# The queries' squares in the output norm: added by GpSimd ahead of the channel sums, or summed by TensorE as groups of their own

## The chip, the cores and the metric

The kernel runs on one core of a Trainium2 chip. The metric is device time in microseconds (us): the median of three runs. The core's engines are TensorE (PE in the profile, with PEld for its weight loads), VectorE (DVE), ScalarE (ACT), GpSimd (POOL) and SyncE (SP), which issues the DMAs. Each engine takes its instructions in the order in which the program lists them, and waits on semaphores for the others.

## The reference: what is computed

Two layers over 1,024 tokens of width 256 (two sequences of 512). Layer 0 is a gated delta rule attention (16 key heads, 32 value heads, head width 128) and a feed-forward layer with ternary weights; layer 1 is an attention with 16 small heads, a ternary feed-forward layer and a mixture of 8 experts. The change lies in the normalisation of layer 0's attention output. Cut to what matters:

```
def _l2norm(x, eps=1e-06):
    return x * jax.lax.rsqrt(jnp.sum(x * x, -1, keepdims=True) + eps)
...
q = _l2norm(q) * Dk ** (-0.5)
k = _l2norm(k)
...
o = _chunk_gated_delta_rule(q, k, v, g, beta)
og = o * jax.nn.silu(z)
og = og * jax.lax.rsqrt(jnp.mean(og * og, -1, keepdims=True) + EPS) * norm_w
return og.reshape(B, T, -1) @ W_out
```

The attention is linear in q, so the kernel never normalises q: it scans with the raw q and takes q's length out in the last norm. With z for the unnormalised `og`, the factor of a token and a value head is then the inverse square root of mean(z*z) plus a constant times (sum of q*q plus a small number). So the sum over the 128 channels of z squared and a scaled sum over the channels of q squared are needed together, for each token and each value head; two value heads share one q.

## The kernel before

Everything is laid out with channels on the 128 partitions and the 512 tokens of a sequence along the free axis. Layer 0's attention is a loop over 16 key heads `h`; a head has two sequences (`seqs`), and a sequence has two units (`s.units`), its value heads. An iteration holds stages of several heads:

- for head `h + 2`: the keys' projection and convolution (`keys_pre`), their norms and decays (`keys`: GpSimd's `rk`, `affine_select` on `e`, and the product `nt<-nt,e` of 128x512), a round trip through DRAM (`base_load`, into `nb`), and `base`, the inversion of 32x32 blocks by 31 steps of two GpSimd instructions each (`xtmp<-xc,nb`, `xc<-xc,xtmp`);
- for head `h + 1`: `inverse`, which fetches those blocks through DRAM (`scr`, `xt`) and joins them into 128x128 inverses with small TensorE products (`bank<-xb,nt` first), and `weights`, which splits the projection weights in a high and a low part (GpSimd makes `wzl`, `wvl`, `wql`, `wkl`);
- for head `h`: projections and convolutions of queries and values, GpSimd's `qg<-qg,q`, the four chunks of `scan`, and `finish`;
- for head `h - 1`: `project` (GpSimd's `ftok`, the inverse square root) and `output`, the product with `W_out`, added into `acc` by VectorE.

`finish` is where the change is. ScalarE squares q in place (with the scale that carries the constant) and writes the squares of each unit's z into a tile `zsq`. Then TensorE sums over the 128 channels by multiplying with ones: the PSUM bank `ps` has 128 rows, 64 for each sequence and in them 32 for each unit, all 32 holding the same sum. Two groups with 64 columns of ones put each sequence's q sum in its 64 rows (`start=True, stop=False`), and four groups with 32 columns add each unit's z sum to its 32 rows. VectorE copies the bank to `zrow`, TensorE transposes it in four pieces, and VectorE makes `tot` from one row of each 32, which GpSimd raises to the power -1/2 (`ftok`).

The order of instructions on each engine isn't the order of this text. All calls go to a recorder (`Plan`), which knows the dependencies and has a cost for every instruction. It then runs a list scheduler many times (`ROUNDS`): each time it places the instructions by priority (the longest path to the end) on the five engines, gives tiles their slots in SBUF and PSUM banks to the groups, keeps the best order that it found, and moves some of the tiles to other slots at random (`SEED`) before the next. The best order is what is issued, from one place, line 572; so every row of the profile has that line, and tiles' names tell the operations apart. TensorE's consecutive matmuls inside `with unit(nc):` are one piece that the scheduler doesn't break up.

Of the kernel before, what the change touches and what calls it, by code (L numbers as in the profile page):

```python
# [42 lines left out]
ALU = mybir.AluOpType  # L43
# [51 lines left out]
def unit(nc):  # L95
    return nc.unit() if isinstance(nc, Plan) else nullcontext()
# [26 lines left out]
class Plan:  # L123
# [7 lines left out]

    BANKS, EARLY, LONG = 8, 3, 4
    CAPS = {"conv": 2}
    ROUNDS, SEED = 120, 9
    SLOTS = (32, 44), (128, 5), (544, 1), (1024, 14), (2048, 50), (3072, 2), (4096, 19), (8192, 3)

    def __init__(self, g):
# [666 lines left out]
def layer0(g, acc, a):  # L804

    nc, tc = g.nc, g.tc
    w_qkvz, w_out = a["w_qkvz"], a["w_out"]
    U = 2 * NC
    with ExitStack() as st:
# [76 lines left out]
        def started(h):  # L886
            seqs = heads[h] = [Seq() for b in range(B)]
            for b, s in enumerate(seqs):
                s.b, s.h, s.units = b, h, []
            return seqs  # L890
# [225 lines left out]
        def finish(h, seqs):  # L1116


            ps = g.psum("lv")
            for s in seqs:  # L1120
                nc.scalar.activation(s.q, s.q, AF.Square, scale=math.sqrt(1e-6) * P)
                for u in s.units:
                    u.sq = ul.tile([P, T], F32, tag="vb", name="zsq", bufs=6)
                    nc.scalar.activation(u.sq, u.z, AF.Square)
            with unit(nc):
                for s in seqs:
                    d = slice(64 * s.b, 64 * s.b + 64)
                    nc.tensor.matmul(ps[d], g.ones[:, :64], s.q, start=True, stop=False)
                for s in seqs:
                    for u in s.units:  # L1130
                        d = 64 * s.b + 32 * u.r
                        nc.tensor.matmul(ps[d : d + 32], g.ones[:, :32], u.sq, start=False, stop=True)
            rows = ul.tile([P, T], F32, tag="a", name="zrow", bufs=2)
            nc.vector.tensor_copy(rows, ps)
            ps = g.psum("lv")
            with unit(nc):
                for c in range(NC):
                    d = slice(c * P, (c + 1) * P)
                    nc.tensor.transpose(ps[:, d], rows[:, d], g.ident)
            tot = ul.tile([P, B, 2, NC], F32, tag="tot", name="tot", bufs=2)  # L1140
            heads = ps.rearrange("p (c b r x) -> p b r c x", c=NC, b=B, r=2)[:, :, :, :, 0]
            nc.vector.tensor_scalar(tot, heads, 1.0 / P, 1e-12 * P, op0=ALU.mult, op1=ALU.add)
            return tot
# [56 lines left out]
        for h in range(HK):  # L1200
            cur = heads[h]
            if h + 2 < HK:
                seqs = started(h + 2)
# [15 lines left out]
            for s in cur:  # L1219
                t = slice(s.b * T, (s.b + 1) * T)  # L1220
                s.z = yl.tile([P, 2, T], F32, tag="z", name="z", bufs=4)
                for u in s.units:
                    ps = g.psum("z")
# [25 lines left out]
            if h:  # L1249
                output(h - 1, done[0], f)  # L1250
            done = cur, finish(h, cur)
            del heads[h]
        output(HK - 1, cur, project(HK - 1, *done))
# [554 lines left out]
```

## Time and profile before

| | us |
|---|---|
| runs | 1270.39, 1272.55, 1276.15 |
| median | 1272.55 |
| the profiled execution, its own time | 1273.35 |
| its span, first to last instruction | 1271.2 |

| engine | busy us | share of span | instructions |
|---|---|---|---|
| TensorE | 1201.5 | 95% | 10452 |
| VectorE | 980.0 | 77% | 2266 |
| ScalarE | 889.1 | 70% | 2347 |
| GpSimd | 794.0 | 62% | 1419 |

The busy shares are averages over the whole span. The page's strip of 40 slices (each about 32 us, the digit is the busy share in tenths) shows how they lie in time:

```profile
PE   5598889999999999999999999999999989999998
POOL 4355777787867878778586858668662366042432
```

The head loop takes the slices from about the sixth to the thirty-second; before it come the gates and the first feed-forward layer, after it layer 1. The four largest groups of GpSimd in the page are its two block-inversion rows, the product `nt<-nt,e` and the small powers:

```profile
L572 POOL TENSOR_TENSOR xtmp<-xc,nb 128x126 f32<-128x126 f32 (+22 forms) x496 | 177.0, 357 | 80.8 <-DMA nb<-scr 21.5
L572 POOL TENSOR_TENSOR xc<-xc,xtmp 128x126 f32<-128x126 f32 (+22 forms) x496 | 186.7, 376 | 31.1
L572 POOL TENSOR_TENSOR ftok<-tot,half 128x16 f32<-128x16 f32 x16 | 46.6, 2912 | 40.1 <-DVE tot L572 40.0
```

After the bar stand the busy time in us and the mean of one in ns; after the next bar the idle time of the engine just before these instructions, and what ended most of it.

### The profile page before, as it was taken

Reading aid. Unit: us, or ns where it says so; the run is one execution under the profiler, and the core shown is the slowest. Engines: PE = TensorE matmul, PEld = TensorE weight load, DVE = VectorE, ACT = ScalarE, POOL = GpSimd, SP = SyncE. Lnnn points to the kernel's source line nnn. Section 1 sums busy time; section 2 is a strip of 40 time slices with the busy share of each in tenths; the row PEclk is TensorE's granted clock in tenths of the full one; section 3 lists DMA queues with packets and bytes.
Section 4 is the critical chain, followed back from the end, with each engine's and each line's share of the span. In section 5 each row is a group of like instructions: output and inputs, shape, how many; then the busy total and the mean of one; then the engine's idle time right before and its main releaser. Section 6 shows DMA issues by size and latency. Waiting matters only on the chain.

```text
span 1271.2 us, 29063 instructions
## 1 busy us (share of the span) xinstructions
PE 1201.5 (95%) x10452; PEld 987.6 (78%) x10452; DVE 980.0 (77%) x2266; ACT 889.1 (70%) x2347; POOL 794.0 (62%) x1419
## 2 busy tenths in 40 slices
PE   5598889999999999999999999999999989999998
PEld 4498777778788888878888888888788777575687
DVE  7975667878897987979888897989776799274363
ACT  6767878687868878776787777777766245756641
POOL 4355777787867878778586858668662366042432
PEclk8799789999999999999999999999999989998999
DMA  6225113234143332332333242333333000000221
GB/s 183 86 66 142 35 35 91 51 92 110 51 109 69 83 77 77 98 84 76 84 84 83 62 110 50 102 80 82 69 89 87 21 9 11 7 6 10 64 68 34
DMA packets 160239, 89.83 MB, mean 71 GB/s; under 512 B 110560, under 2 KB 142368, under 8 KB 160096
## 3 DMA queue, kind: packets, MB, share of 16 engines
q1 hardware_dynamic: 160096, 87.97, 27.3%
q8 instruction: 83, 1.36, 0.4%
q14 instruction: 60, 0.49, 0.1%
HBM read 78.07 MB, written 9.73 MB: 69 GB/s over the span
## 4 chain that ended last, share of the span: by engine, by line
PE 68%; DVE 15%; ACT 8%; POOL 5%; issue 2%; DMA 2%; SPq 0%; DVEq 0%; POOLq 0%; ACTq 0%
PE bank L572 68%; DVE v L572 2%; DVE xb L572 2%; DVE q L572 1%; ACT e L572 1%; POOL xc L572 1%; POOL xtmp L572 1%; DVE acc L572 1%; ACT nt L572 1%; DVE q_wa L572 1%; ACT L572 1%; DVE cc L572 1%; DVE vb L572 1%; ACT bank L572 1%; ACT v L572 1%
## 5 line engine op out<-in xcount | busy, mean ns | idle before, releaser
L572 POOL TENSOR_TENSOR xtmp<-xc,nb 128x126 f32<-128x126 f32 (+22 forms) x496 | 177.0, 357 | 80.8 <-DMA nb<-scr 21.5
L572 POOL TENSOR_TENSOR xc<-xc,xtmp 128x126 f32<-128x126 f32 (+22 forms) x496 | 186.7, 376 | 31.1
L572 DVE SCALAR_TENSOR_TENSOR v<-bank,conv,v 128x511 f32<-128x511 f32 (+2 forms) x192 | 141.2, 741 | 8.1 <-ACT v L572 6.2
L572 PE MATMUL bank<-wo,z 128*128 128x256 f32 x512 | 124.9, 384 | 3.0 <-DVE v L572 2.5
L572 PE MATMUL bank<-e,v 128*128 128x128 f32 (+4 forms) x768 | 118.2, 333 | 0.3 <-ACT v L572 0.3
L572 DVE SCALAR_TENSOR_TENSOR acc<-bank,ftok,acc 128x256 f32<-128x256 f32 x256 | 108.6, 474 | 7.3 <-PE bank L572 4.5
L572 PEld LDWEIGHTS bank<-wo,z 128*128 128x128 f32 x512 | 94.4, 192 | 16.6 <-DVE v L572 2.9
L572 ACT ACTIVATE v<-bank,ckd 128x128 f32<-128x128 f32 x192 | 59.8, 366 | 44.4 <-PE bank L572 43.8
L572 PEld LDWEIGHTS bank<-e,v 128*128 128x128 f32 (+1 forms) x768 | 83.4, 165 | 8.1 <-issue 3.4
L572 DVE SCALAR_TENSOR_TENSOR k<-bank,conv,k 128x511 f32<-128x511 f32 (+2 forms) x96 | 70.4, 739 | 20.2 <-ACT k L572 19.6
L572 ACT ACTIVATE v<-bank,cc 128x128 f32<-128x128 f32 x256 | 80.4, 374 | 5.9 <-PE bank L572 5.6
L572 POOL TENSOR_TENSOR nt<-nt,e 128x512 f32<-128x512 f32 x60 | 76.2, 1285 | 9.6 <-ACT nt L572 8.7
L572 PEld LDWEIGHTS bank<-vb,xt 128*128 128x128 f32 x512 | 73.2, 192 | 11.2 <-DVE wo L572 1.7
L572 PE MATMUL bank<-vb,xt 128*128 128x128 f32 x512 | 79.1, 279 | 0.9 <-DVE vb L572 0.9
L572 ACT ACTIVATE e<-e,ngc 128x128 f32<-128x128 f32 x256 | 76.7, 388 | 4.4 <-POOL e L572 4.2
L572 PE MATMUL bank<-qg,st 128*128 128x128 f32 x384 | 75.8, 279 | 1.1 <-DVE vb L572 0.4
L572 POOL TENSOR_TENSOR rk<-kss,half 128x4 f32<-128x4 f32 x32 | 33.0, 1030 | 66.5 <-DVE kss L572 54.8
L572 DVE SCALAR_TENSOR_TENSOR q<-bank,conv,q 128x511 f32<-128x511 f32 (+2 forms) x96 | 70.9, 743 | 3.5 <-ACT q L572 2.5
L572 POOL TENSOR_TENSOR ftok<-tot,half 128x16 f32<-128x16 f32 x16 | 46.6, 2912 | 40.1 <-DVE tot L572 40.0
L572 PEld LDWEIGHTS bank<-qg,st 128*128 128x128 f32 x384 | 63.4, 192 | 7.3 <-issue 1.6
L572 DVE SCALAR_TENSOR_TENSOR vb<-bank,neg,vb 128x128 f32<-128x128 f32 x192 | 57.9, 342 | 12.0 <-PE bank L572 11.0
L572 PEld LDWEIGHTS bank<-xb,nt 32*32 32x32 f32 (+1 forms) x1536 | 52.5, 118 | 17.5 <-issue 5.4
(329 smaller groups left out, 3843.8 us busy)
## 6 DMA issues: line engine op xcount, KB each, us to landing
e<-rows SPq DMA_DIRECT2D x64, 256.0 KB
raw<-in_w_qkvz SPq DMA_DIRECT2D x48, 256.0 KB
qg<-rows SPq DMA_DIRECT2D x32, 384.0 KB
nb<-scr SPq DMA_DIRECT2D x32, 256.0 KB
xc<-in_consts SPq DMA_DIRECT2D x16, 256.0 KB
wo<-in_w_out SPq DMA_DIRECT2D x16, 256.0 KB
scr<-nt SPq DMA_DIRECT2D x128, 32.0 KB
scr<-xc SPq DMA_DIRECT2D x32, 128.0 KB
```

Source lines behind the costliest of these rows:

```text
L572: call(*map(placed, args), **{k: placed(x) for k, x in kwargs.items()})
```

## The change

GpSimd adds the squared q into each unit's `zsq`, in place, right after ScalarE has made it: four additions of 128x512 f32 a head. The two TensorE groups over q go away, and the four groups over `zsq` now start their rows themselves. What is summed is the same. The scheduler's number of rounds and its seed are other ones.

```
-    ROUNDS, SEED = 120, 9
+    ROUNDS, SEED = 70, 11
...
                 for u in s.units:
                     u.sq = ul.tile([P, T], F32, tag="vb", name="zsq", bufs=6)
                     nc.scalar.activation(u.sq, u.z, AF.Square)
+                    nc.gpsimd.tensor_tensor(u.sq, u.sq, s.q, ALU.add)
             with unit(nc):
-                for s in seqs:
-                    d = slice(64 * s.b, 64 * s.b + 64)
-                    nc.tensor.matmul(ps[d], g.ones[:, :64], s.q, start=True, stop=False)
                 for s in seqs:
                     for u in s.units:
                         d = 64 * s.b + 32 * u.r
-                        nc.tensor.matmul(ps[d : d + 32], g.ones[:, :32], u.sq, start=False, stop=True)
+                        nc.tensor.matmul(ps[d : d + 32], g.ones[:, :32], u.sq, start=True, stop=True)
```

## The prediction, made before the changed kernel ran

> **What bounds the kernel now.** I read the page's busy line and chain first, then busy time by stage, then the rows around the edited sums, last GpSimd's queue.
>
> From the page, busy time and the chain's shares by engine:
>
> ```profile
> PE 1201.5 (95%) x10452; PEld 987.6 (78%) x10452; DVE 980.0 (77%) x2266; ACT 889.1 (70%) x2347; POOL 794.0 (62%) x1419
> PE 68%; DVE 15%; ACT 8%; POOL 5%; issue 2%; DMA 2%; SPq 0%; DVEq 0%; POOLq 0%; ACTq 0%
> ```
>
> TensorE is busy for 95% of the span and makes 68% of the chain. GpSimd is at 62%, but that is an average, so stages matter (each row: stretch, its length, then busy time and instructions of PE, PEld, DVE, ACT, POOL, then clock, DMA share, GB/s):
>
> ```profile
> 300.00:350.00 50.00, 47.49 (x466) 39.31 (x465) 43.04 (x89) 39.25 (x101) 42.18 (x73) 1.00 0.31 86
> 550.00:600.00 50.00, 49.07 (x441) 40.16 (x440) 41.45 (x92) 37.94 (x106) 41.48 (x75) 1.00 0.32 75
> 700.00:750.00 50.00, 50.00 (x516) 42.31 (x506) 43.59 (x94) 37.87 (x103) 34.69 (x70) 1.00 0.27 63
> 850.00:900.00 50.00, 48.53 (x471) 40.11 (x469) 39.76 (x86) 37.02 (x105) 40.33 (x73) 1.00 0.26 66
> 950.00:1010.00 60.00, 58.97 (x555) 49.94 (x554) 40.94 (x100) 30.47 (x78) 14.71 (x9) 1.00 0.26 70
> ```
>
> In the head loop TensorE has almost no holes: over the fourteen 50 us stretches from 250 to 950 it idles 9.7 us in all, from 0 to 2.51 us each. So TensorE time that is removed there comes off the end, unless something else takes over. GpSimd is at 32 to 42 us of each 50 in the loop, not at 62%.
>
> **What is removed.** Three rows in order of time on TensorE (start us, length us) around one head's sums:
>
> ```profile
> 868.88 1.08 PE L572 MATMUL bank<-q,allc 128*64 128x512 f32 x4
> 869.89 1.06 PE L572 MATMUL bank<-zsq,allc 128*32 128x512 f32 x8
> 870.88 0.50 PE L572 MATMUL bank<-xl,wzh 128*128 128x512 f32 x1
> ```
>
> The two groups over the queries are four records here (a matmul in full precision leaves two). From their start to the start of the zsq sums is 1.01 us; the four zsq groups take another 0.99 and stay. The same 1.01 stands between the starts at the other heads I looked at (271.32 to 272.33, 551.39 less 550.38), but 1.81 at the first head (226.16 to 227.97). 16 heads by 1.01 make 16.2 us; the group's total by form is 18.1 us busy (64 records), the upper bound. I take **-16.2**. All sixteen lie at 226 to 1000, where TensorE is busy 97 to 100%, so I count them whole. ScalarE's squares, the row copy and the transposes are unchanged.
>
> **What is added.** GpSimd gets 4 adds a head of 128x512 f32, 64 in all. The nearest row is its multiply of the same shape and type:
>
> ```profile
> L572 POOL TENSOR_TENSOR nt<-nt,e 128x512 f32<-128x512 f32 x60 | 76.2, 1285 | 9.6 <-ACT nt L572 8.7 <-ACT e L572 0.7
> ```
>
> 64 x 1.285 = 82.2 us of busy time, 5.14 a head. What hides it is GpSimd's idle time. From 200 to 950 it is busy 563.8 us and idle 186.2; its listed waits in that stretch sum to 129.7 us, led by
>
> ```profile
> POOL rk L572 <- DVE kss L572: 35.7, 13, 9.5
> POOL xtmp L572 <- DMA nb<-scr: 21.5, 6, 4.6
> POOL xtmp L572 <- DMA xc<-in_consts: 19.3, 3, 8.9
> ```
>
> and the other 56.5 us are hand-overs of some 0.05 us between its roughly 1,090 instructions. The heads end 51.4 us apart (226 to 998, 15 steps), so 750 us hold 14.6 heads: 58 adds by 1.285 + 0.05, 78 us. They fit into the 129.7, with 52 us left, and 37 once the stretch is 15 us shorter: 5%. GpSimd is then nearly as full as TensorE, on an in-order queue that must still wait for DMA and VectorE in places.
>
> **Who is queued behind the adds.** GpSimd runs the chain that inverts the 32x32 blocks (xc, xtmp), and the block inverse on TensorE follows it closely:
>
> ```profile
> 945.09 0.23 POOL L572 TENSOR_TENSOR xc<-xc,xtmp 128x16 f32<-128x16 f32 x1
> ```
>
> For the fifteen heads from 1 on, TensorE's first block product starts 11.1 to 19.0 us after the chain's last step (here at 958.16, 12.8 later), mean 13.9. The DMAs to DRAM and back plus three transposes fill most of that, so only about 2.8 us a head are slack over the least case. An add placed inside the chain delays it by 1.34 us, four by 5.3. But GpSimd's own time between the ends of two chains has room: the fourteen intervals are 42 to 69 us with 4.8 to 12.5 us free after busy time and hand-overs, and only one (554.8 to 606.8) has less than 5.3. Late chains make late inverses, then late scans; TensorE covers that with other heads' projections and outputs as long as it has some.
>
> An added wait: each add waits for ScalarE's square of z and stands ahead of nt, qg, ftok and the weight splits. Behind the sums, the row copy, transposes, tot and ftok move later by up to two adds (2.7 us); they feed only the next head's output, so I count nothing, and if that cover failed it would be 16 x 2.7 = 43 us. At the last head the squares end at 996.92 and GpSimd idles, so two adds end near 999.1 against 998.75 for the start of the old zsq sums: +0.4.
>
> To price the crowding I set TensorE's holes against GpSimd's load. In the three stretches with GpSimd over 40 us (300, 550, 850) TensorE idled 2.51, 0.93 and 1.47, mean 1.64. If every one of the fourteen stretches becomes like these, that is 14 x 1.64 - 9.7 = +13. If none does, 0. No row tells more; I take the middle, **+6**. The whole order is drawn anew too (another seed, fewer rounds), and the built program differs on TensorE nearly from its first row. Its price is bounded by the stretches: all with no hole, -9.7; all like the worst, 14 x 2.51 - 9.7 = +25. I take 0, for the sign is unknown, and keep both ends.
>
> VectorE: in this trace a tiny operation grew beside a GpSimd operation:
>
> ```profile
> 872.64 1.30 POOL L572 TENSOR_TENSOR wvl<-raw,wvh 128x512 fp32r<-128x512 f32 x1
> 872.83 1.12 DVE L572 TENSOR_TENSOR r<-rk 128x4 f32<-128x4 f32 x1
> ```
>
> The 128x4 product took 1.12 us, ending with GpSimd's split, against 0.146 at its least; such products are four kinds by 32 in the kernel. If the adds raise GpSimd's share from 0.75 to 0.86, and half of an add's 1.285 is lost on each meeting, it is 128 x 0.11 x 0.64 = 9 us of VectorE time over the run, on an engine at 77%; from 0 to 9, I take 0 for the end, and it lies inside the range.
>
> The Trainium skill ("SBUF — State Buffer", section "Who interferes with whom") says that a VectorE instruction with two inputs in SBUF and a GpSimd instruction that reads SBUF exclude each other for the whole instruction. The row above agrees (1.12 us beside the split). By that rule, with every add blocking one such instruction for its full length, VectorE would lose at most 64 x 1.285 = 82 us, spread over a loop in which it is not the bound; the sum above doesn't use it.
>
> **The sum.** -16.2 + 6 + 0.4 = about -10. The profiled execution took 1273.35 (span 1271.2 and 2.2 around it), 0.8 above the median of 1272.55, so I go from the median: **1262**. Own range of this case: 1253 (crowding 0, first-head gain) to 1269 (crowding 13).
>
> **The rivals.**
> 1. *GpSimd sets the pace (slower).* The adds land inside the block chain and aren't absorbed, and the inverse, with 2.8 us of slack a head, goes late. For it: chains and inverses are tied at every head, and 5% of free time is little for an in-order queue that waits on DMAs. Against it: TensorE had filler in all stretches, and the free time per interval covers the adds. The price is 1.34 us for each add that isn't absorbed; it decides once more than 16.2 / 1.34 = 12 of the 64 adds' time reaches TensorE. With a third of them, 21 x 1.34 = 28: 1272.5 - 16.2 + 28 = 1284.
> 2. *The gain is eaten in place (no change).* Holes of the size seen at GpSimd's busiest, plus a less lucky order of about 3 us: 1272.5 - 16.2 + 13 + 3 = 1272. For it: the best stretches (0 idle at 700 to 750) are those with little GpSimd work.
> 3. *The whole gain and a better order.* -16.2 with half of the 9.7 us of holes closed: 1251. For it: TensorE's load falls in each head alike. Against it: GpSimd's load rises most where it is fullest.
> That the change frees no TensorE time can be left out: the two groups have their own 1.01 us slot.
>
> **How the numbers follow.** Forecast (partial gain, 1253 to 1269) 0.42; rival 3 (below 1253) 0.11; rival 2 (1266 to 1279, less the part counted above) 0.19; rival 1 (above 1279) 0.28. A measurement of this kernel tells about 0.5% from no change, 6.4 us: below 1266.2 is faster, above 1278.9 slower. Of the forecast's 0.42, 0.04 lie above 1266, giving faster 0.49, same 0.23, slower 0.28. The range 1250 to 1287 leaves out some 0.07 below and 0.12 above. Both signs hold much of the chance; the likeliest case's own range stands above.
>
> **What would show it.** Right: no q sums before the zsq sums; 64 adds near 1.29 us each; TensorE's busy time about 16 us lower; GpSimd at 41 to 44 of each 50 us in the loop; TensorE's idle time in 250 to 950 near 16 us. Wrong: that idle time above 30 us with block products waiting for xc through the DMAs (rival 1), GpSimd's adds above 1.5 us, or TensorE's holes below 6 us (rival 3).

## The result, and the profile after

| | median us | runs | ratio to before, 95% interval |
|---|---|---|---|
| before, beside it | 1273.88 | 1270.39 to 1276.15 | |
| changed | 1327.75 | 1319.34 to 1330.47 | 1.0414 [1.0361, 1.0468] |

The change costs 4%; 1262 was predicted, with a range to 1287. The profiled execution took 1330.47 us, with a span of 1328.6. Its busy line and chain by engine, from the page:

```profile
PE 1219.3 (92%) x10388; PEld 1007.8 (76%) x10388; DVE 993.1 (75%) x2266; ACT 888.5 (67%) x2347; POOL 869.9 (65%) x1483
PE 61%; DVE 18%; ACT 8%; DMA 6%; POOL 3%; issue 2%; SPq 1%; DVEq 0%; ACTq 0%; POOLq 0%
```

TensorE has 64 records fewer, worth 16 us, and yet is busy 18 us longer; its idle time grew from 70 to 109 us. GpSimd has its 64 additions (81 us, its busy time grows by 76) and a smaller share of the chain than before, 3% for 5%. What came into the chain is DMA, 6% for 2%. The additions are as long as forecast, but GpSimd stands idle ahead of them (its rows by form, and its waits):

```profile
L572 POOL TENSOR_TENSOR zsq<-zsq,q 128x512 f32<-128x512 f32 x64 | 81.4, 1281 | 38.3 <-ACT zsq L572 33.2 <-PE bank L572 5.1
```

By stage (columns as in the prediction):

```profile
300.00:350.00 50.00, 48.87 (x481) 41.25 (x480) 41.35 (x93) 41.75 (x114) 39.25 (x61) 1.00 0.36 91
500.00:550.00 50.00, 45.61 (x417) 37.49 (x418) 39.40 (x87) 34.81 (x93) 39.40 (x74) 0.86 0.14 33
550.00:600.00 50.00, 45.07 (x448) 37.78 (x447) 37.43 (x80) 33.96 (x90) 40.78 (x67) 0.97 0.34 86
700.00:750.00 50.00, 48.31 (x383) 42.09 (x382) 45.92 (x99) 36.26 (x96) 44.58 (x88) 0.97 0.35 83
```

TensorE now has a few us of holes in nearly every stretch, and the clock granted to it is below 1.00 in nine of the fourteen stretches from 250 to 950 us. There it idles 40.7 us, where 9.7 stood before. I added up 2 us stretches over the head loop, from the first head's sums to the last's (228 to 999 before, 229 to 1050 after): idle time 11.2 us before and 41.6 after; busy time lost to low clock (busy time by one less the granted clock) 0.9 and 24.1. That is +30 and +23. With the 16 us removed this would make +37 of the loop's +50; the other 13 is work of other stages that the new order put into the loop, above all output products (`bank<-wo,z`: 468 records in that stretch for 412, worth 14 us).

One such hole, close up: the changed kernel's busy time in 4 us stretches.

```profile
490.00:494.00 4.00, 4.00 (x27) 3.69 (x26) 3.85 (x9) 3.90 (x15) 3.06 (x3) 1.00 0.95 241
494.00:498.00 4.00, 4.00 (x38) 4.00 (x37) 1.93 (x5) 3.97 (x10) 1.70 (x3) 1.00 0.98 235
498.00:502.00 4.00, 0.61 (x6) 0.42 (x4) 0.00 (x0) 1.27 (x4) 2.39 (x2) 0.96 0.56 134
502.00:506.00 4.00, 1.70 (x46) 1.46 (x48) 3.63 (x8) 1.35 (x4) 3.60 (x8) 0.50 0.33 83
506.00:510.00 4.00, 4.00 (x61) 2.90 (x58) 3.23 (x8) 2.68 (x7) 1.47 (x3) 0.50 0.00 0
510.00:514.00 4.00, 4.00 (x87) 3.11 (x80) 2.84 (x7) 2.03 (x5) 3.61 (x9) 0.50 0.01 4
514.00:518.00 4.00, 4.00 (x30) 2.50 (x30) 2.73 (x6) 3.30 (x10) 0.55 (x2) 0.84 0.00 0
```

The DMA engines are full (0.95, 0.98) for 8 us. Then VectorE stands still and TensorE with it, and after the hole it works at half clock from 502 to 515. What stood in SyncE's queue (start, length, operation):

```profile
488.58 1.01 SPq L572 DMA_DIRECT2D e<-rows  x2
489.64 0.43 SPq L572 DMA_DIRECT2D qg<-rows  x1
490.12 0.93 SPq L572 DMA_DIRECT2D e<-rows  x2
491.10 0.68 SPq L572 DMA_DIRECT2D qg<-rows  x1
491.82 1.41 SPq L572 DMA_DIRECT2D xc<-in_consts  x1
493.27 8.99 SPq L572 DMA_DIRECT2D xt<-scr  x8
```

The eight small fetches of a head's inverted blocks (32 KB each) come behind seven transfers of 256 and 384 KB for later heads. VectorE's transposes, which wait for their first part, start at 502.18, and TensorE's block products follow at once:

```profile
502.76 1.43 PE L572 MATMUL bank<-xb,nt 32*32 32x32 f32 x32 [4.15 <-DVE xb L572]
```

Over the run TensorE waits 22.5 us for `xb` in 13 such places, against 2.4 us in three before (total, times, longest; before, then after):

```profile
PE bank L572 <- DVE xb L572: 2.4, 3, 1.7
```

```profile
PE bank L572 <- DVE xb L572: 22.5, 13, 4.1
```

From a head's first fetch to TensorE's first block product the DMA share is 0.45 before and 0.66 after, on the mean of the fifteen heads from 1 on; from the first fetch to the first transpose it takes 4.9 and 5.9 us. The strips of DMA share by slice show the difference at a glance, before and after:

```profile
DMA  6225113234143332332333242333333000000221
```

```profile
DMA  5225122414151431315142341423313000000220
```

Before has an even load through the loop; after has bursts of 4 and 5 with 1 between.

### The profile page after: what moved, and what is told of

It reads as the page before. It is cut to its first block, busy times and chain, and to the rows that moved or that the text cites. A ratio compares the mean times of both kernels' runs of the same rounds, so it can differ in the third digit from the quotient of the medians.

```text
span 1328.6 us, 29014 instructions
## 1 busy us (share of the span) xinstructions
PE 1219.3 (92%) x10388; PEld 1007.8 (76%) x10388; DVE 993.1 (75%) x2266; ACT 888.5 (67%) x2347; POOL 869.9 (65%) x1483
## 4 chain that ended last, share of the span: by engine, by line
PE 61%; DVE 18%; ACT 8%; DMA 6%; POOL 3%; issue 2%; SPq 1%; DVEq 0%; ACTq 0%; POOLq 0%
PE bank L572 61%; DMA xt<-scr 4%; DVE xb L572 2%; DVE v L572 2%; DVE q L572 2%; ACT nt L572 2%; DVE acc L572 2%; SPq L572 1%; ACT e L572 1%; POOL xc L572 1%; ACT v L572 1%; DVE q_wa L572 1%; DVE xn L572 1%; DMA e<-rows 1%; DMA scr<-xc 1%
## 5 line engine op out<-in xcount | busy, mean ns | idle before, releaser
L572 POOL TENSOR_TENSOR xc<-xc,xtmp 128x126 f32<-128x126 f32 (+22 forms) x496 | 184.6, 372 | 30.6
L572 DVE SCALAR_TENSOR_TENSOR v<-bank,conv,v 128x509 f32<-128x509 f32 (+2 forms) x192 | 140.4, 741 | 11.0 <-ACT v L572 9.3
L572 PE MATMUL bank<-wo,z 128*128 128x256 f32 x512 | 129.2, 391 | 3.2 <-DVE acc L572 2.8
L572 POOL TENSOR_TENSOR zsq<-zsq,q 128x512 f32<-128x512 f32 x64 | 81.4, 1281 | 38.3 <-ACT zsq L572 33.2
L572 PEld LDWEIGHTS bank<-xb,nt 32*32 32x32 f32 (+1 forms) x1536 | 57.8, 126 | 50.8 <-DVE xb L572 15.5
L572 PE MATMUL bank<-xb,nt 32*32 32x32 f32 (+1 forms) x1536 | 66.6, 212 | 30.8 <-DVE xb L572 22.5
L572 ACT ACTIVATE nt<-bank,ncc 128x128 f32<-128x128 f32 x240 | 64.3, 390 | 3.5 <-DVE ncc L572 2.2
```

Of the source, the lines that this page charges most:

```text
L572: call(*map(placed, args), **{k: placed(x) for k, x in kwargs.items()})
```

## The experiments

Two causes lay open: A, the additions on GpSimd; B, the order that the scheduler drew anew with other sums, seed and rounds. In the code `...` stands for lines left out. All medians are of four runs or more, ratios are to the kernel before on the same chip.

**The draw and the sums, one at a time.** e1 and e2 cross the two kernels:

```
e1, in before:   -    ROUNDS, SEED = 120, 9        +    ROUNDS, SEED = 70, 11
e2, in changed:  -    ROUNDS, SEED = 70, 11        +    ROUNDS, SEED = 120, 9
```

> The old sums (six groups on TensorE, no additions on GpSimd) with the changed kernel's rounds and seed (70, 11). Theory A, the additions stand at the head of GpSimd's queue, wait for ScalarE's squares and hold up the block chain behind them: another draw of the order costs little, 1262 to 1290 us, and GpSimd's waits show no zsq. Theory B, the new draw found a worse order: 1310 to 1335 us, near the changed kernel's 1328.

Measured: 1335.37 us, 1.0473 [1.0439, 1.0506]. No addition in it, and slower than the changed kernel.

> The changed sums (additions on GpSimd, four groups) with the rounds and seed of before (120, 9). Theory A: slow again, 1305 to 1340 us, with 25 us or more of GpSimd's idle time before the additions. Theory B: 1255 to 1275 us.

Measured: 1336.4 us, 1.0486 [1.0455, 1.0516], with 30.6 us of idle time before the additions. Each fits the theory that says "slow", so neither alone decides: the old seed doesn't save the new sums, and the new draw ruins the old ones.

**The order held fast.** e3, e5 and e6 plan the kernel before as it is, with its costs, and edit only what is issued. The four engines other than GpSimd get their instructions in the order of before.

```
e3: nc.adds.append([squared, nc.ops[-1], (u.sq, u.sq, s.q), 0, sums])
    ...
    del nc.ops[-1].calls[:2]          # the unit of the sums loses its two query groups
    ...
    for x in [x for x in self.adds if x[0] in done and x[1] in done]:   # both squares issued
        ...
        self.adds.remove(x)
        real_add(*map(placed, x[2]), ALU.add)
e5: the `del` alone, no additions
e6: as e3, the additions just ahead of the unit of the sums
```

In all three the four groups over `zsq` start their rows themselves.

> The order, slots and banks planned for the kernel before are kept; only at the issue the two query groups are left out of TensorE's unit and each addition is put on GpSimd right behind the instruction that stood there when ScalarE's squares were issued. So the change without any new planning. Theory A: the additions wait and delay the chain, 1290 to 1340 us. Theory B: 1255 to 1270 us, the 16 us of TensorE less a little. If both hold in part: 1275 to 1290.

> The order, slots and banks of before; TensorE's two query groups a head are not issued and nothing is added (the sums lack the queries' squares). Theory C, the removal is worth what TensorE's rows say and the loss in e3 is GpSimd's additions alone: 1252 to 1264 us. Theory D, any shift of that finely fitted order loses its gain: 1268 to 1320 us.

> As e3, but each head's four additions stand on GpSimd as late as they can, just ahead of the issue of TensorE's sums. If what cost 50 us in e3 was GpSimd waiting for ScalarE's squares with the block chain behind it, GpSimd's idle time before zsq falls from 25 us to under 8, and the time to 1270 to 1300 us, though TensorE now waits for the additions at the sums (up to 16 x 5 us). If the 82 us of work alone is what costs: 1315 to 1345 us.

Measured: e3 1324.04 us, 1.0404 [1.0368, 1.0439]; e5 1264.24 us, 0.9933 [0.9911, 0.9954]; e6 1330.94 us, 1.0441 [1.041, 1.0472]. So in the old order the removal is worth 9 us, and the additions then cost 60. The chains by engine of e5 and of e3 show who came into the path:

```profile
PE 57%; DVE 19%; ACT 14%; POOL 5%; issue 3%; DMA 1%; SPq 0%; DVEq 0%; ACTq 0%; POOLq 0%
```

```profile
PE 43%; POOL 23%; DVE 13%; ACT 9%; issue 6%; DMA 4%; SPq 1%; POOLq 0%; DVEq 0%; ACTq 0%
```

GpSimd goes from 5% to 23%. One path by which it gets there is the inverse square root behind the sums: VectorE's additions into `acc` wait for `ftok` 35.7 us in e3, against 4.3 in e5.

```profile
DVE acc L577 <- POOL ftok L577: 35.7, 11, 7.0
```

e6 put the additions where they needn't wait for the squares. GpSimd's idle time ahead of them fell from 25.2 us (e3) to 0.6, but the time didn't fall, so waiting for the squares isn't by itself what costs. In e6 TensorE's weight loads waited for the additions, about as long as e6 is slower than e5 (67 us):

```profile
PEld bank L577 <- POOL zsq L575: 68.6, 60, 3.0
```

So neither place suits: early, the additions hold up GpSimd's other chains, late, the sums on TensorE. An order that was fitted to a GpSimd without the additions has little room for their 82 us: from e5 to e3 GpSimd's busy time rose by 76.7 us and its idle time fell by only 16.0, so the span grew by 60.7. A place between the two wasn't tried.

**The new order without the additions.** e4 plans the changed kernel as it is and doesn't issue the additions (`nc.ops[-1].calls.clear()` behind them).

> The changed kernel's order, slots and banks, but the 64 additions are not issued: the sums lack the queries' squares. Theory A: without them the chain runs freely, 1265 to 1295 us. Theory B: the order itself is slow, 1305 to 1328 us.

Measured: 1330.14 us, 1.0441 [1.0415, 1.0467]. The order planned around the additions is as slow without them. TensorE's longest wait there is the same one:

```profile
PE bank L572 <- DVE xb L572: 20.4, 17, 3.1
```

In the head loop it idles 32.5 us and loses 36.7 to low clock. So theory B holds for this order as it stands: its holes at the block products don't come from the additions being executed. GpSimd's idle time says the same: with the additions (the changed kernel) it is 74 us less than without them (e4), so in the order that was planned for them they do fit into its waits.

**How much of a draw is luck.** e8, e10 and e12 change only rounds or seed of the kernel before, e11 those of the changed one.

```
e8:  ROUNDS, SEED = 114, 9     e10: ROUNDS, SEED = 120, 4     e12: ROUNDS, SEED = 120, 8
e11: ROUNDS, SEED = 120, 24    (the changed kernel)
```

> The kernel before with 114 rounds in place of 120: the same search, stopped before its last find, so an order that the scheduler itself holds for 5 us longer (1253.1 in place of 1247.8 by its own costs). If the chip follows the scheduler's ranking: 1275 to 1285 us. If the order of before is a lucky one on the chip beyond that: 1295 to 1340 us, with the changed kernel and e1.

> The old sums with 120 rounds and seed 4, an order that the scheduler's own costs put at 1250.7 us, near the 1247.8 of before. If the scheduler's figure tells what the chip does and the old sums are no luck of one seed: 1270 to 1290 us. If the order of before has luck that its figure does not hold: 1300 to 1340 us.

> The new sums with 120 rounds and seed 24, the best of 24 seeds by the scheduler's costs (1256.8; the changed kernel's order has 1262.5). If the draw is most of the loss: 1285 to 1315 us. If the additions cost in any order: 1315 to 1340 us.

> The old sums with 120 rounds and seed 8, an order with 1265.9 us by the scheduler's costs, a middling one of eleven seeds and near the changed kernel's 1262.5. If the draw is what costs: 1305 to 1340 us, as slow as the changed kernel without any addition. If the additions are: 1275 to 1295 us.

Measured: e8 1276.02, 1.0012 [0.9997, 1.0028]; e10 1312.6, 1.031 [1.026, 1.036]; e11 1310.22, 1.0266 [1.0229, 1.0302]; e12 1296.29, 1.0171 [1.0115, 1.0227]. e8 lies where the scheduler's ranking put it, e10 where the order of before has luck beyond its figure, and e11 where the draw is most of the loss; e12 falls between its two ranges, 1 us above the one for the additions. The old sums take 1273, 1296, 1313 and 1335 us by seed, and the scheduler's figure doesn't rank them: 1250.7 gave 1312.6, 1265.9 gave 1296.3. The kernel before is the lucky one of four; e8, an earlier find of the same search, shares its luck. How rare such an order is, four seeds don't tell.

**The crowd of transfers.** e9 takes the changed kernel's order and moves only DMAs within SyncE's queue:

```
for op in order[first : last + 1]:       # from a head's first scr<-xc to its last xt<-scr
    late = op.engine == "SP" and op not in group and not op.opens
    if late:
        behind.append(op)
        continue
    ...                                   # released early where a later instruction needs it
    stay.append(op)
order[first : last + 1] = stay + behind
```

> The changed kernel with one edit at the issue: between the first DMA that writes a head's blocks out of xc and the last that fetches them into xt, the other DMAs on SyncE's queue (e, qg, nb, xc, raw, wo) go behind the fetches where no instruction between needs them. Orders of the other four engines, slots and banks stay. Theory E, the holes of TensorE before the block products come from big transfers queued ahead of the blocks, and each hole brings low clock after it: the share of the DMA engines during the fetches falls from 0.67 to under 0.5, TensorE's waits for xb from 22 us to under 8, the time to 1285 to 1310 us. If the transfers don't matter, or the big ones come too late now: 1320 to 1345 us.

Measured: 1348.32 us, 1.0561 [1.0532, 1.059]. Half a hit: the share of the DMA engines during the fetches fell to 0.50 and TensorE's wait for `xb` to 8 us, but the loop got longer, with 48.7 us idle and 45.6 lost to low clock. Its waits by TensorE:

```profile
PE bank L589 <- DVE xb L589: 8.1, 5, 4.0
PE bank L589 <- DVE acc L589: 7.9, 8, 3.3
```

The holes moved: now later instructions came late. Pushing a transfer behind helps only if the rest of the order expects it there. That is what e13 to e18 do: the scheduler is told of the crowd and plans anew.

```
-            return (480.0, 2700.0 + size / 105.0) if size < 1 << 19 else (max(480.0, size / 260.0), 3000.0)
+            return max(480.0, size / 235.0), 2700.0 + size / 105.0 if size < 1 << 19 else 3000.0
```

> The changed kernel (70 rounds, seed 11) with one edit in the scheduler's prices: a DMA holds SyncE's place in the plan for its bytes at 235 GB/s, at least 0.48 us, so that transfers issued together are planned one behind the other (235 to 241 GB/s is what the trace showed with all sixteen DMA engines busy). This draws another order; by its own costs it has 1276.1 us. If crowding is what the chip added in the drawn orders, the chip now follows the plan: 1290 to 1312 us, and the share of the DMA engines during block fetches falls below 0.55. If not: 1320 to 1345 us.

> The old sums with 120 rounds and seed 4 and that price for crowding (1261.4 us by its costs); without it this seed took 1312.6. If crowding is the cause: 1275 to 1298 us. If not: 1305 to 1330 us.

> The kernel before with that price for crowding, same rounds and seed (1268.7 us by its costs). If crowding is the cause: 1280 to 1300 us, close to the other seeds, since nothing of this seed's luck is left. If not: anything from 1270 to 1335 us.

> The old sums with 70 rounds and seed 11 and that price for crowding (1269.0 us by its costs); without it this draw took 1335.4 (e1). If crowding is the cause: 1280 to 1305 us. If not: 1315 to 1340 us.

Measured: e13 1314.88, 1.0311 [1.0267, 1.0355]; e14 1289.59, 1.0113 [1.0093, 1.0132]; e15 1289.77, 1.012 [1.0098, 1.0142]; e16 1298.48, 1.0177 [1.0153, 1.0201]. For the old sums all three fall where theory "crowding" put them, within 9 us of each other, and 21 to 30 us over the scheduler's figure; seeds 4 and 11 gained 23 and 37 us, the lucky seed 9 lost 16. The range of e15 lies inside the one for "if not", so of these three only e14 and e16 could have spoken against the theory. e13 misses by 3 us.

The crowd itself hardly changed. During the fetches the DMA share is 0.66 in e13, as in the changed kernel; 0.66 in e14, as in e10; 0.68 in e16 for 0.72 in e1. What changed is that TensorE has other work meanwhile: its wait for `xb` is 1.9 us in e13 (22.5 in the changed kernel), 6.3 in e14 (15.2 in e10) and 1.7 in e16 (14.3 in e1). Yet e13 still idles 40 us in the head loop and loses 32 to low clock, at holes spread over many waits. So the waits at the block products are a part of a slow draw and not the whole. Another price is also another draw, and other draws alone moved the old sums by up to 62 us; that all of e14's and e16's gain comes from the price isn't shown.

> The new sums with the price for crowding, 120 rounds, seed 12: the best of thirteen seeds by the scheduler's costs, 1269.6 us, equal to e15 and e16 of the old sums (1289.8 and 1298.5 us on the chip). If the new sums cost nothing beyond the plan: 1288 to 1302 us. If the chip adds to them (additions that wait on GpSimd, its fuller queue): 1306 to 1325 us.

> As e17 with seed 11, 1271.7 us by the scheduler's costs. If the new sums cost nothing beyond the plan: 1290 to 1304 us. If the chip adds to them: 1308 to 1325 us.

Measured: e17 1327.55, 1.0434 [1.0364, 1.0505]; e18 1314.88, 1.0333 [1.0257, 1.041]. Both are on the slow side of their expectations, e17 3 us beyond its range. At figures equal to e15 and e16 the new sums take some 27 us more than the old (means 1321 and 1294). Against the scheduler's figures, the new sums took 39 to 58 us more (e13, e17, e18), the old ones 21 to 30 (e14 to e16). So the chip does add to them beyond the plan, as far as so few draws can tell; e18 is the search of e13 taken 50 rounds further, and no draw of its own. In e17 GpSimd stood 64.4 us idle ahead of the additions, in e18 29.7 us, in e13 37.2; that this is what costs isn't shown.

| order | old sums, us | new sums, us |
|---|---|---|
| seeds run, scheduler as it was | 1273, 1296, 1313, 1335 | 1310, 1328, 1336 |
| their mean | 1304 | 1325 |
| crowding priced | 1290, 1290, 1298 | 1315, 1315, 1328 |
| their mean | 1293 | 1319 |

## Why the prediction was wrong

- **The bound:** right. TensorE sets the end, and the removed groups leave it: 64 records fewer. In a held order that was worth 9 us (e5), not 16.2: with it the loop's holes grew from 11.2 to 16.5 us, and low clock cost 5.4 in place of 0.9. The term was mis-sized, as a removal opens holes that others must fill in time.
- **"They fit into the 129.7, with 52 us left":** right for the order that ran, wrong for the order that it was worked out from. In the changed kernel's order the additions cost nothing that the runs show: 1327.75 us with them and 1330.14 without (e4; ratios 1.0414 and 1.0441, with intervals that overlap). In the old order, from whose rows the 129.7 was read, they cost 60 us (e3 less e5): a wait was counted as room wherever it lay, but the additions come when the squares are ready, its largest wait stayed (`rk` for `kss`, 59.5 us in e5 and 59.9 in e3), and 25.2 us of new ones came ahead of the additions. In drawn orders the new sums take some 21 to 26 us more (the table's means). With the scheduler as it was, that is less than single draws differ, so it isn't clear of chance; with crowding priced, the three new draws, from two searches, all lie above the three old ones.
- **"They feed only the next head's output, so I count nothing":** in the old order this cover failed. VectorE's waits for `ftok` went from 4.3 to 35.7 us (e5, e3), where the prediction's price for that case was 43 us of time; how much of the 60 us it makes isn't shown. In the changed kernel they are 1.6 us.
- **The order drawn anew, taken as 0 with bounds -9.7 and +25:** the step that failed, and by e1 and e4 enough for the whole loss. The bounds came from the holes of one good order, each priced at its own length. Drawing anew alone cost the old sums 19 to 61 us (e12, e10, e1), with more holes and with half clock behind many of them, and the order of before was the best of the four that ran. The mean of its four seeds is 31 us above it. With the some 21 us between the sums' means this makes 52 of the 54 measured, which says only that the changed kernel is an ordinary draw of the new sums.
- **Rival 1** had the sign, and GpSimd setting the pace shows in e3, though TensorE waits for `xb` only 3.3 us there. Its signature, TensorE idle over 30 us with block products waiting through the DMAs, is what the changed kernel shows; yet e4 has it without the additions. So for the changed kernel the cause that rival 1 names isn't shown. For the old order its price was too low: 60 us is 45 of the 64 additions at 1.34 us, where it took a third.
- **VectorE beside GpSimd, 0 to 9 us:** too low as busy time. In one and the same order VectorE is busy 970.7 us without the additions (e4) and 993.1 with them, 22 us more; as the time is the same, it cost nothing there.
- **Shown and not shown:** that the draw alone can cost the whole loss is shown (e1), and that the changed kernel's order is as slow without the additions (e4); so is that the additions cost 60 us in the old order (e3 against e5). What makes one draw slower than another stays open in part: that late block fetches are one cause is supported by the changed kernel's holes, e14 and e16, and limited by e9, e13 and e15. How much of the 54 us the new sums cost in drawn orders, beside the luck of the old draw, is an estimate from means over few draws. No version ran faster than before, save e5, which leaves out the queries' squares.

## What to carry to other kernels

Where a scheduler searches for an order at random, compare a change over several draws of both versions, or hold the order fast; one draw against one draw mixes the change with luck (here 62 us between seeds). Idle time on an in-order engine is not free room: ask for each idle stretch what it waits for, and whether the new instruction is ready at that time. Of some 77 us of additions an order planned for them hid 74 in GpSimd's idle time (the changed kernel beside e4), an order held fast 16 (e3 beside e5). A hole on the bound engine has to be priced with what its clock does afterwards.

## What the runs showed of the hardware

Holes of TensorE cost more than their length. In the changed kernel a hole of 4.15 us (to 502.76) was followed by a granted clock of 0.50 from 501.7 to 515.3, one of 3.38 (to 568.88) from 569.9 to 573.3, one of 2.44 (to 623.94) from 624.5 to 634.8; one of 1.85 (to 263.30) left it at 1.00. The Trainium skill ("TensorE: Matmul & The Clock Gate", section "Part 1: The HAM clock gate (the "warmup" mystery)") says that the clock is halved after an idle window of about 3.4 us and restored after about as much sustained work. The length agrees, but the window need not be wholly idle: here holes of 2.2 to 2.4 us were enough, and the way back took 3.4 to 13.7 us, with smaller holes on the way counted in.

The trace shows why length alone doesn't decide. The 44 changes of the clock that stretches of 1 us place over the whole span all lie on one fixed grid with steps of 3.41 us (501.66, 515.32, 569.92, 573.34, 624.54 and 634.78 are 0, 4, 20, 21, 36 and 39 steps from the first of them). The hole of 1.85 us lies across an edge of the grid and leaves TensorE busy for 2.13 and 2.65 us of two steps; one of 2.17 us, to 268.87, falls into a single step, leaves 1.25, and half clock follows:

```profile
259.32:262.73 3.41, 2.13 (x12) 1.00 0.98 242
262.73:266.14 3.41, 2.65 (x50) 1.00 0.09 12
266.14:269.56 3.42, 1.25 (x81) 1.00 0.02 5
269.56:272.97 3.41, 3.41 (x12) 0.50 0.00 0
```

(Columns: stretch, its length, TensorE's busy time and instructions, clock, DMA share, GB/s.) In the changed kernel's head loop all six steps at full clock with less than 2.1 us of busy time were followed by half clock, those with 2.1 to 2.8 us went either way, and each of the nine returns to full clock came after a step that was busy for 3.3 us or more. The bound isn't sharp: in e1 a step of 1.78 us kept full clock.

Eight fetches of 32 KB behind a burst of larger transfers took 8.9 us to the first use, where the mean before is 4.9, while the DMA engines moved 235 to 241 GB/s at a share of 0.95 to 0.98. That isn't a ceiling: other 4 us stretches of the same trace, at shares of 0.90 and more, show 173 to 317 GB/s. So the 235 GB/s that e13 to e18 plan with are a rough price.
